# Rows 1 to 4 as one tile in an outer-product batch norm: a new order of tiles and one run for four rows

## The chip, the cores and the metric

The kernel runs on one core of a Trainium2 chip. The metric is the device time of one execution in microseconds (us); of several, the median is taken. The kernel before takes 1877.3 us (four runs, 1877.24 to 1877.37).

## What is computed

`r_xi` and `r_xj` hold 1024 samples of 39 fields of 16 numbers. For every pair of fields (row r, column c, c < r: 741 pairs) the 16 x 16 outer product is formed, normalised over the batch and the 256 places of that pair, scaled, and multiplied by a weight:

```python
cross = xj[:, rows, :, None] * xi[:, cols, None, :]
mean = jnp.mean(cross, axis=(0, 2, 3), keepdims=True)
var = jnp.mean(jnp.square(cross - mean), axis=(0, 2, 3), keepdims=True)
normed = (cross - mean) * jax.lax.rsqrt(var + BN_EPS)
normed = normed * gamma[None, :, None, None] + beta[None, :, None, None]
out = normed[:, :, None, :, :] * W[None, None, :, :, :]
```

The output is float32, 1024 x 741 x 256: 777 MB. In it, a sample's pairs lie row by row: row r has r pairs and begins at pair r(r-1)/2, so rows 1, 2, 3, 4 are pairs 0 to 9, next to each other. One pair is 1024 bytes.

## The kernel before

Samples lie on 128 partitions, eight on each. For about the first 35 us the inputs are loaded and mean and variance of all pairs are worked out from sums and a Gram matrix of the fields (TensorE, DVE, ACT, POOL); this gives for each pair a scale s (`st_sb[:, 0]`) and a shift t (`st_sb[:, 1]`). These are spread to all partitions in groups of rows (`ROW_GROUPS`); each group has a tile number at which its last three DVE steps (`apply`) are done.

Then the output is made in tiles. A tile is one row r for T = 2 samples of each partition, so each row has four tiles (sample pairs t0 = 0, 2, 4, 6) of 2 r pairs. The list `tiles` (lines 67 to 76) gives their order and their place in the buffer `y_sb`, which has two slots of 2 x 38 pairs. From row 38 down, a slot takes the tile of row r and, behind it, that of row 38 - r, so that it is full; then the other slot follows. First come rows 19, 20 and 18. The end is row 21 with row 17.

A tile passes three steps, and the main loop (lines 525 to 533) writes them out in the order that each engine keeps:

- `scale_xi` (L163): POOL multiplies xi by s into `xs` (L169), two tiles ahead; `xs` has two buffers.
- `products` (L177): for each of the two samples, 16 instructions multiply `xs` by one number of xj: 11 or 12 of them on ACT (L147), 5 or 4 on POOL (L149). They write all r pairs of that sample, so they wait until the stores of what lay there before have landed. For rows 1 to 4 (`SHORT`) DVE does it alone: one scaling (L182) and one product for each sample (L192).
- `finish` (L256): the shift is added and the weight multiplied, on DVE in one instruction for each pair and both samples (L293). Some pairs go elsewhere: in tiles of rows over 33 (`long`), ACT adds the shift of 8 pairs (L277) and POOL multiplies them, 4 pairs at a time (L282); in the others, POOL does both (L279, L282) for 13% of the pairs; in rows 1 to 4, DVE does all.

`store` (L205) then issues the runs on SP's queue (L216), which keeps their order. Rows over 30 go out in pieces (`bounds`), rows over 19 sample by sample, the others with both samples in one DMA. One DMA spreads over the 16 DMA engines; each run of one sample in one partition is one packet. Row 37 and row 38 go as a first piece of both samples and then a second piece for each; rows 36 to 31 as a first piece of sample 0, the rest of sample 0, and the whole of sample 1. A tile of row r can begin in a slot when sample 0's runs have left it, and finish its products when sample 1's have.

Of the kernel before, what the change touches and what calls it, by code (L numbers as in the profile page):

```python
# [7 lines left out]
F32 = mybir.dt.float32  # L8
AF = mybir.ActivationFunctionType
ALU = mybir.AluOpType  # L10
# [4 lines left out]
T = 2  # L15
# [3 lines left out]
ONE, LONG, WHOLE = 30, 33, 36  # L19
# [6 lines left out]
POOL_SHARE, POOL_PAIRS_LONG, POOL_PAIRS_FIRST = 0.13, 8, 3  # L26

LOADS = (1, 2, 3, 4, 6, 8)

SHORT, OWN = 4, 2  # L30


ROW_GROUPS = (
    (19, 20, 0, None), (20, 21, 1, None), (18, 19, 1, 2), (38, 39, 1, 8), (34, 38, 1, 9), (1, 5, 1, 10), (29, 34, 2, 36),
    (5, 10, 2, 37), (25, 29, 3, 76), (10, 14, 3, 77), (21, 25, 4, 108), (14, 18, 4, 109),
)
SHORT_GROUP = 5

# [2 lines left out]
def tile_pair_outer_batchnorm(  # L41
# [15 lines left out]
    nc = tc.nc  # L57
    P = nc.NUM_PARTITIONS
    NB, F, E = xi.shape
    NT = NB // P  # L60
    EE = E * E
    NP = F * (F - 1) // 2
    first = [r * (r - 1) // 2 for r in range(F)]

    half = T * (F - 1)
    mid = (F - 1) // 2
    tiles = [(mid, t0, t0 // T * half // 2) for t0 in range(0, NT, T)]
    slot = 0  # L70
    for r in (mid + 1, *range(F - 1, mid + 1, -1)):
        for t0 in range(0, NT, T):
            tiles.append((r, t0, slot * half))
            if r < F - 1:
                tiles.append((F - 1 - r, t0, slot * half + T * r))
            slot ^= 1

    RAW = 1

    cpool = ctx.enter_context(tc.tile_pool(name="cpool", bufs=1))  # L80
    scaled_short = ctx.enter_context(tc.tile_pool(name="scaled_short", bufs=1))
    scaled = ctx.enter_context(tc.tile_pool(name="scaled", bufs=2))
    psp = ctx.enter_context(tc.tile_pool(name="ps", bufs=1, space=bass.MemoryType.PSUM))
    xi_sb = cpool.tile([P, NT, F, E], F32, name="xi_sb")
# [47 lines left out]
    xj_short = ps_c.rearrange("p (t r i) -> p t r i", t=NT, i=E)  # L132
# [4 lines left out]
    def view(n):  # L137
        r, _, u = tiles[n]
        return y_sb[:, u : u + T * r, :].rearrange("p (t n) e -> p t n e", t=T)

    def product(n, engine, t, i, src):

        r, t0, _ = tiles[n]
        y = view(n).rearrange("p t n (i j) -> p t n i j", j=E)[:, t, :, i, :]
        scale = xj_sb[:, t0 + t, r, i : i + 1]
        if engine is nc.scalar:
            nc.scalar.activation(y, src, AF.Copy, scale=scale)  # L147
        else:
            engine.tensor_scalar(y, src, scale, 1.0, ALU.mult, ALU.mult)  # L149
# [7 lines left out]
    def emit(work, count):  # L157
        for _, step in zip(range(count), work):
            step()

    xs_of = {}

    def scale_xi(n):  # L163
        r, t0, _ = tiles[n]
        if r <= SHORT:
            return
        n0 = first[r]
        xs = scaled.tile([P, T, r, E], F32, tag="xs", name=f"xs_{r}_{t0}")
        nc.gpsimd.tensor_tensor(  # L169
            xs,  # L170
            xi_sb[:, t0 : t0 + T, 0:r, :],
            s_sb[:, :, n0 : n0 + r, :].to_broadcast([P, T, r, E]),
            ALU.mult,
        )
        xs_of[n] = xs

    def products(n):  # L177

        r, t0, _ = tiles[n]
        if r <= SHORT:  # L180
            xs = scaled_short.tile([P, T, r, E], F32, tag="xs_short", name=f"xs_{r}_{t0}")
            nc.vector.tensor_tensor(  # L182
                xs,
                xi_sb[:, t0 : t0 + T, 0:r, :],
                s_short[:, first[r] : first[r] + r]
                .unsqueeze(1)
                .unsqueeze(3)
                .to_broadcast([P, T, r, E]),
                ALU.mult,
            )  # L190
            for t in range(T):
                nc.vector.tensor_tensor(  # L192
                    view(n)[:, t].rearrange("p n (i j) -> p n i j", j=E),
                    xs[:, t].unsqueeze(2).to_broadcast([P, r, E, E]),
                    xj_short[:, t0 + t, r - 1 : r, :].unsqueeze(3).to_broadcast([P, r, E, E]),
                    ALU.mult,
                )
            return
        xs = xs_of.pop(n)
        split = E - (POOL_I_FIRST[n] if n < 3 else POOL_I_LONG if tiles[n][0] > LONG else POOL_I)  # L200
        for t in range(T):
            for i in range(E):
                product(n, nc.scalar if i < split else nc.gpsimd, t, i, xs[:, t])

    def store(n, c0, c1, t_from=0, t_to=T):  # L205
        r, t0, _ = tiles[n]
        n0 = first[r]

        whole = n >= len(FIRST_PIECES) and r <= WHOLE
        step = 1 if r > mid and (whole or c1 == r) else t_to - t_from  # L210
        for t in range(t_from, t_to, step):
            if whole and step == 1 and t == t_to - 1:
                if c1 < r:
                    continue
                c0 = 0
            nc.sync.dma_start(  # L216
                out_v[:, t0 + t : t0 + t + step, (n0 + c0) * EE : (n0 + c1) * EE],
                view(n)[:, t : t + step, c0:c1, :].rearrange("p t n e -> p t (n e)"),
            )
# [14 lines left out]
    def weigh(n):  # L234

        y = view(n)
        for c0, c1 in zip(bounds(n), bounds(n)[1:]):
            affine(n, range(c0, min(c1, OWN)), (nc.vector,))
            nc.vector.tensor_tensor(  # L239
                y[:, :, c0:c1, :],  # L240
                y[:, :, c0:c1, :],
                w_dve.unsqueeze(1).to_broadcast([P, T, c1 - c0, EE]),
                ALU.mult,
            )
            store(n, c0, c1)

    def bounds(n):
        if n < len(FIRST_PIECES):
            return FIRST_PIECES[n]
        r = tiles[n][0]  # L250
        if r <= ONE:
            return 0, r

        return 0, r // 2 + max(0, (WHOLE + 1 - r) * 3 // 2), r

    def finish(n):  # L256


        r = tiles[n][0]
        n0 = first[r]  # L260
        y = view(n)
        long = r > LONG
        p1 = r // 2 if long else r
        if long:
            share = POOL_PAIRS_LONG
        elif RAW < n < 10:
            share = POOL_PAIRS_FIRST
        else:
            share = int(r * POOL_SHARE + 0.5) if r > SHORT else 0
        p0 = p1 - share  # L270
        step = POOL_PAIRS_LONG // 2 if long else r
        for c0 in range(p0, p1, step):
            c1 = min(c0 + step, p1)
            for c in range(c0, c1):
                t_c = t_sb[:, n0 + c : n0 + c + 1]
                if long:
                    nc.scalar.activation(y[:, :, c, :], y[:, :, c, :], AF.Identity, bias=t_c)  # L277
                else:
                    nc.gpsimd.tensor_scalar(  # L279
                        y[:, :, c, :], y[:, :, c, :], t_c, 1.0, ALU.add, ALU.mult  # L280
                    )
            nc.gpsimd.tensor_tensor(  # L282
                y[:, :, c0:c1, :],
                y[:, :, c0:c1, :],
                w_sb.unsqueeze(1).to_broadcast([P, T, c1 - c0, EE]),
                ALU.mult,
            )

        size = 1 if n == RAW else T
        for t in range(0, T, size):  # L290
            for c0, c1 in zip(bounds(n), bounds(n)[1:]):
                for c in [*range(c0, min(c1, p0)), *range(max(c0, p1), c1)]:
                    stt(  # L293
                        y[:, t : t + size, c, :],
                        y[:, t : t + size, c, :],
                        t_sb[:, n0 + c : n0 + c + 1],
                        w_dve.to_broadcast([P, size, EE]),
                        ALU.add,
                        ALU.mult,
                    )  # L300
                store(n, c0, c1, t, t + size)

    with tc.manual_schedule():
# [209 lines left out]

        affine(0, range(OWN, 12))
        scale_xi(1)
        affine(0, range(12, mid))
        weigh(0)
        for group in range(1, len(ROW_GROUPS)):
            spread(group)
        s_short = spread_of[SHORT_GROUP][0][:, 0]  # L520
        apply(1)
        products(1)
        scale_xi(2)

        for n in range(1, len(tiles)):
            if n + 2 < len(tiles):
                scale_xi(n + 2)
            finish(n)
            for group, (_, _, _, tile_of) in enumerate(ROW_GROUPS):
                if n == tile_of:  # L530
                    apply(group)
            if n + 1 < len(tiles):
                products(n + 1)
            if n == 12:
                nc.scalar.copy(xj_short, xj_sb[:, :, 1 : SHORT + 1, :])
# [28 lines left out]
```

## Time and profile before

| | us |
|---|---|
| median of four runs | 1877.3 |
| profiled execution | 1877.23 |
| its span, first to last instruction | 1875.5 |
| DVE busy | 1723.9 |
| ACT busy | 1647.3 |
| POOL busy | 1535.6 |
| store queue's packets, share of 16 DMA engines over the span | 98.1% |

In the page, part 1 has each engine's busy time, part 2 the span in 40 slices (busy share in tenths; GB/s moved), part 3 the DMA queues. q1 is the queue of the loads and stores that SP issues, q10 ACT's loads, q14 the fetching of instructions. In a row of a group or of the timeline, "128x528" is partitions x elements, "xN" a count; the bracket or the part behind the second bar tells the idle time ahead of it and what ended it. A row of an answer on waits reads: who waited, for what, us in total, times, the longest. A row of a DMA issue ends in the time from the issue to the landing on the last of the 16 engines.

### The profile page before, as it was taken

The numbers are of one execution on the slowest core, as the hardware profiler recorded it, in microseconds if no ns is written. First come the engines' busy times: TensorE is split into PE (matmuls) and PEld (weight loads), VectorE is DVE, ScalarE is ACT, GpSimd is POOL, SyncE is SP. The second block draws the span as 40 slices with busy tenths as digits, with TensorE's granted clock in tenths as the row PEclk, the third lists the DMA queues.
The fourth block names the chain that finished last, engine by engine and source line by source line (L and its number), as shares of the span: only waits on it lengthen the run. The fifth ranks groups of instructions, "written<-read, shape, count | busy, mean of one in ns | idle before, by whom it ended". The sixth has DMA issues, their size and how long they took to land. (4 is left out here: it accounts for less than half of the span.)

```text
span 1875.5 us, 9638 instructions
## 1 busy us (share of the span) xinstructions
PE 26.0 (1%) x130; PEld 23.3 (1%) x130; DVE 1723.9 (92%) x2640; ACT 1647.3 (88%) x3416; POOL 1535.6 (82%) x1746
## 2 busy tenths in 40 slices
PE   4000000000000000000000000000000000000000
PEld 4000000000000000000000000000000000000000
DVE  8999888899999999999999999999999999999994
ACT  7999888898888899989999999998999998989892
POOL 8999877787777788888888888888888888888882
DMA  5999999999999999999999999999999999999998
GB/s 198 387 422 419 431 424 425 426 425 426 425 426 425 426 426 426 431 426 420 424 425 432 426 425 432 425 425 432 425 430 425 430 426 429 426 428 431 427 428 349
DMA packets 54714, 783.63 MB, mean 418 GB/s; under 512 B 4720, under 2 KB 6384, under 8 KB 17520
## 3 DMA queue, kind: packets, MB, share of 16 engines
q1 hardware_dynamic: 53344, 779.72, 98.1%
q10 hardware_dynamic: 1296, 3.29, 0.5%
q14 instruction: 73, 0.60, 0.1%
q8 instruction: 1, 0.02, 0.0%
HBM read 6.00 MB, written 776.99 MB: 417 GB/s over the span
## 5 line engine op out<-in xcount | busy, mean ns | idle before, releaser
L293 DVE SCALAR_TENSOR_TENSOR y_sb<-y_sb,st_sb,w_dve 128x512 f32<-128x512 f32 (+1 forms) x2511 | 1653.2, 740 | 115.3 <-issue 101.4
L147 ACT ACTIVATE y_sb<-xs,xj_sb 128x288 f32<-128x288 f32 (+20 forms) x3194 | 1515.6, 581 | 177.7 <-DMA out_dram<-y_sb 145.9
L149 POOL TENSOR_SCALAR y_sb<-xs,xj_sb 128x480 f32<-128x480 f32 (+27 forms) x1126 | 607.2, 565 | 8.4 <-DMA out_dram<-y_sb 8.4
L282 POOL TENSOR_TENSOR y_sb<-y_sb,w_sb 128x2048 f32<-128x2048 f32 (+3 forms) x155 | 517.7, 3346 | 89.9 <-ACT y_sb L277 80.3
L169 POOL TENSOR_TENSOR xs<-xi_sb,st_sb 128x640 f32<-128x640 f32 (+33 forms) x135 | 184.2, 1364 | 198.1 <-ACT y_sb L147 194.3
L279 POOL TENSOR_SCALAR y_sb<-y_sb,st_sb 128x512 f32<-128x512 f32 x291 | 197.6, 695 | 5.1 <-ACT y_sb L147 5.1
L277 ACT ACTIVATE y_sb<-y_sb,st_sb 128x512 f32<-128x512 f32 x160 | 100.3, 711 | 4.0 <-POOL y_sb L149 2.3
L192 DVE TENSOR_TENSOR y_sb<-xs,ps 128x256 f32<-128x256 f32 (+3 forms) x32 | 24.8, 818 | 0.6
L491 PE MATMUL ps<-y_sb 39*128 39x38 f32 (+37 forms) x76 | 16.4, 397 | 2.8 <-DVE y_sb L477 2.8
L491 PEld LDWEIGHTS ps<-y_sb 39*128 39x128 f32 x76 | 16.3, 329 | 3.1 <-DVE y_sb L477 3.1
L355 ACT ACTIVATE y_sb<-y_sb 128x1248 f32<-128x1248 f32 x8 | 10.0, 1245 | 2.8 <-POOL y_sb L344 2.4
L360 DVE TENSOR_REDUCE y_sb<-y_sb 128x78 f32<-128x1248 f32 x8 | 11.2, 1446 | 0.3 <-ACT y_sb L355 0.3
L147 ACT ACTIVATE y_sb<-xi_sb,xj_sb 128x304 f32<-128x304 f32 x24 | 11.4, 540 | 0.0
L344 POOL TENSOR_TENSOR y_sb<-xi_sb,y_sb 128x1248 f32<-128x1248 f32 x4 | 9.2, 2321 | 2.4 <-ACT y_sb L393 2.4
L239 DVE TENSOR_TENSOR y_sb<-y_sb,w_dve 128x2048 f32<-128x2048 f32 (+4 forms) x6 | 10.7, 1839 | 0.1
L334 DVE TENSOR_REDUCE y_sb<-xi_sb 128x39 f32<-128x624 f32 (+1 forms) x6 | 6.1, 1012 | 3.9 <-DMA xi_sb<-in_r_xi_dram 3.9
L344 POOL TENSOR_TENSOR y_sb<-xj_sb,y_sb 128x1248 f32<-128x1248 f32 x4 | 9.2, 2320 | 0.0
L380 PE MATMUL ps<-y_sb 128*39 128x79 f32 x48 | 8.0, 340 | 15.3 <-DVE y_sb L360 15.1
L232 POOL TENSOR_SCALAR y_sb<-y_sb,st_sb 128x512 f32<-128x512 f32 x8 | 6.5, 816 | 2.1 <-ACT y_sb L147 2.1
L334 DVE TENSOR_REDUCE y_sb<-xj_sb 128x39 f32<-128x624 f32 (+1 forms) x6 | 6.1, 1016 | 0.9 <-DMA xj_sb<-in_r_xj_dram 0.9
L230 ACT ACTIVATE y_sb<-y_sb,st_sb 128x512 f32<-128x512 f32 x9 | 6.5, 804 | 0.2 <-ACT y_sb L147 0.2
L380 PEld LDWEIGHTS ps<-y_sb 128*39 128x39 f32 x48 | 5.8, 178 | 17.3 <-DVE y_sb L360 10.5
(59 smaller groups left out, 37.5 us busy)
## 6 DMA issues: line engine op xcount, KB each, us to landing
out_dram<-y_sb SPq DMA_DIRECT2D x16, 3072.0 KB, 21.9
out_dram<-y_sb SPq DMA_DIRECT2D x20, 2432.0 KB, 12.5
out_dram<-y_sb SPq DMA_DIRECT2D x10, 4608.0 KB, 15.1
out_dram<-y_sb SPq DMA_DIRECT2D x12, 3840.0 KB, 21.6
out_dram<-y_sb SPq DMA_DIRECT2D x16, 2816.0 KB, 22.3
out_dram<-y_sb SPq DMA_DIRECT2D x12, 3584.0 KB, 23.1
out_dram<-y_sb SPq DMA_DIRECT2D x12, 3328.0 KB, 24.3
out_dram<-y_sb SPq DMA_DIRECT2D x15, 2560.0 KB, 11.9
```

The source lines that it names most:

```text
L147: nc.scalar.activation(y, src, AF.Copy, scale=scale)
L149: engine.tensor_scalar(y, src, scale, 1.0, ALU.mult, ALU.mult)
L169: nc.gpsimd.tensor_tensor(xs, xi_sb[:, t0 : t0 + T, 0:r, :], s_sb[:, :, n0 : n0 + r, :].to_broadcast([P, T, r, E]), ALU.mult,)
L192: nc.vector.tensor_tensor(view(n)[:, t].rearrange("p n (i j) -> p n i j", j=E), xs[:, t].unsqueeze(2).to_broadcast([P, r, E, E]), xj_short ...
L277: nc.scalar.activation(y[:, :, c, :], y[:, :, c, :], AF.Identity, bias=t_c)
L279: nc.gpsimd.tensor_scalar(y[:, :, c, :], y[:, :, c, :], t_c, 1.0, ALU.add, ALU.mult)
L282: nc.gpsimd.tensor_tensor(y[:, :, c0:c1, :], y[:, :, c0:c1, :], w_sb.unsqueeze(1).to_broadcast([P, T, c1 - c0, EE]), ALU.mult,)
L293: stt(y[:, t : t + size, c, :], y[:, t : t + size, c, :], t_sb[:, n0 + c : n0 + c + 1], w_dve.to_broadcast([P, size, EE]), ALU.add, ALU.mult,)
L334: nc.vector.tensor_reduce(total[:, t0:t1, part(x)], sources[x][:, t0:t1], AX.X, ALU.add)
L344: nc.gpsimd.tensor_tensor(devs[n % 7], sources[x][:, t0 : t0 + T], shift[:, x : x + 1, :].unsqueeze(3).to_broadcast([P, T, F, E]), ALU.sub ...
L380: nc.tensor.matmul(ps_g[acc][0:F, 0 : 2 * F + 1], lhs, fb[:, t], start=t == 0, stop=t == NT - 1)
L491: nc.tensor.matmul(ps[:, :, first[r] - n0 : first[r] - n0 + r], pick[:, r, :], stq[:, :, 0:r], start=True, stop=True,)
```

## The change

The tiles get another order, and rows 1 to 4 become one.

- Rows 1 to 4 of a sample pair are one tile of 10 pairs (`grouped`; row number 0 in the list of short tiles, 10 in `tiles`). DVE makes the four rows' products as before, one after another, into that tile; `finish` does its 10 pairs on DVE; its store is one DMA in which a run is 10 pairs long, from pair 0.
- Rows 37, 36, 35, 34 have no short tile behind them. Rows 33 to 29 keep rows 5 to 9. In each of rows 28, 27, 26, 25 the first sample pair's slot takes a grouped tile; the other three slots take the tiles of rows 10, 11 and 12 in order (10, 10, 10 beside 28; 10, 11, 11 beside 27; 11, 11, 12 beside 26; 12, 12, 12 beside 25). Rows 24 to 21 take rows 13 to 16, so their slots hold 37 pairs a sample.
- Row 17's four tiles come last, two in each slot.
- The long tile beside a grouped one (`beside`) is finished as rows over 33 are: 8 pairs over ACT and POOL.
- In `ROW_GROUPS` six tile numbers are changed to suit the order.

```diff
 ROW_GROUPS = (
-    (19, 20, 0, None), (20, 21, 1, None), (18, 19, 1, 2), (38, 39, 1, 8), (34, 38, 1, 9), (1, 5, 1, 10), (29, 34, 2, 36),
-    (5, 10, 2, 37), (25, 29, 3, 76), (10, 14, 3, 77), (21, 25, 4, 108), (14, 18, 4, 109),
+    (19, 20, 0, None), (20, 21, 1, None), (18, 19, 1, 2), (38, 39, 1, 8), (34, 38, 1, 9), (1, 5, 1, 10), (29, 34, 2, 26),
+    (5, 10, 2, 27), (25, 29, 3, 64), (10, 14, 3, 65), (21, 25, 4, 96), (14, 18, 4, 97),
 )
...
-    tiles = [(mid, t0, t0 // T * half // 2) for t0 in range(0, NT, T)]
+    rest = SHORT * (SHORT + 1) // 2
+    samples = range(0, NT, T)
+    tiles = [(mid, t0, t0 // T * half // 2) for t0 in samples]
+    short = [(mid - 1, t0) for t0 in samples]
+    short += [(r, t0) for r in range(SHORT + 1, rest) for t0 in samples]
+    late = [(r, t0) for r in range(rest, mid - 2) for t0 in samples]
+    for q, t0 in enumerate(samples):
+        late.insert(4 * q, (0, t0))
+    short += late
+
+    grouped, beside = set(), set()
     slot = 0
     for r in (mid + 1, *range(F - 1, mid + 1, -1)):
-        for t0 in range(0, NT, T):
+        for t0 in samples:
             tiles.append((r, t0, slot * half))
-            if r < F - 1:
-                tiles.append((F - 1 - r, t0, slot * half + T * r))
+            if r < F - SHORT - 1 and (short[0][0] or rest) < F - r:
+                row, t1 = short.pop(0)
+                if not row:
+                    beside.add(len(tiles) - 1)
+                    grouped.add(len(tiles))
+                tiles.append((row or rest, t1, slot * half + T * r))
             slot ^= 1
+    for q, t0 in enumerate(samples):
+        tiles.append((mid - 2, t0, (slot ^ q // 2) * half + q % 2 * T * (mid - 2)))
...
+    def base(n):
+        return 0 if n in grouped else first[tiles[n][0]]
...
-        if r <= SHORT:
-            xs = scaled_short.tile([P, T, r, E], F32, tag="xs_short", name=f"xs_{r}_{t0}")
...
-            for t in range(T):
+        if n in grouped:
+            for row in range(1, SHORT + 1):
+                pairs = slice(first[row], first[row] + row)
+                xs = scaled_short.tile([P, T, row, E], F32, tag="xs_short", name=f"xs_{row}_{t0}")
                 nc.vector.tensor_tensor(
...
+                for t in range(T):
+                    nc.vector.tensor_tensor(
+                        view(n)[:, t, pairs].rearrange("p n (i j) -> p n i j", j=E),
+                        xs[:, t].unsqueeze(2).to_broadcast([P, row, E, E]),
+                        xj_short[:, t0 + t, row - 1 : row, :].unsqueeze(3).to_broadcast([P, row, E, E]),
+                        ALU.mult,
+                    )
             return
...
     def store(n, c0, c1, t_from=0, t_to=T):
         r, t0, _ = tiles[n]
-        n0 = first[r]
+        n0 = base(n)
...
-        n0 = first[r]
+        n0 = base(n)
         y = view(n)
-        long = r > LONG
+        long = r > LONG or n in beside
...
-            share = int(r * POOL_SHARE + 0.5) if r > SHORT else 0
+            share = 0 if n in grouped else int(r * POOL_SHARE + 0.5)
```

More of the change, by code (lines that the diff above doesn't have):

```diff
@@ L68, in tile_pair_outer_batchnorm @@
     mid = (F - 1) // 2
-    tiles = [(mid, t0, t0 // T * half // 2) for t0 in range(0, NT, T)]
+    rest = SHORT * (SHORT + 1) // 2
[8 more added lines that the diff above has]
+    grouped, beside = set(), set()
     slot = 0
     for r in (mid + 1, *range(F - 1, mid + 1, -1)):
-        for t0 in range(0, NT, T):
+        for t0 in samples:
             tiles.append((r, t0, slot * half))
-            if r < F - 1:
-                tiles.append((F - 1 - r, t0, slot * half + T * r))
+            if r < F - SHORT - 1 and (short[0][0] or rest) < F - r:
[4 more added lines that the diff above has]
+                tiles.append((row or rest, t1, slot * half + T * r))
             slot ^= 1
+    for q, t0 in enumerate(samples):
+        tiles.append((mid - 2, t0, (slot ^ q // 2) * half + q % 2 * T * (mid - 2)))
+    assert not short
     RAW = 1
@@ L179, in products @@
         r, t0, _ = tiles[n]
-        if r <= SHORT:
-            xs = scaled_short.tile([P, T, r, E], F32, tag="xs_short", name=f"xs_{r}_{t0}")
[L182 to L190, printed above, removed]
-            for t in range(T):
+        if n in grouped:
+            for row in range(1, SHORT + 1):
+                pairs = slice(first[row], first[row] + row)
+                xs = scaled_short.tile([P, T, row, E], F32, tag="xs_short", name=f"xs_{row}_{t0}")
                 nc.vector.tensor_tensor(
-                    view(n)[:, t].rearrange("p n (i j) -> p n i j", j=E),
-                    xs[:, t].unsqueeze(2).to_broadcast([P, r, E, E]),
-                    xj_short[:, t0 + t, r - 1 : r, :].unsqueeze(3).to_broadcast([P, r, E, E]),
+                    xs,
+                    xi_sb[:, t0 : t0 + T, 0:row, :],
+                    s_short[:, pairs].unsqueeze(1).unsqueeze(3).to_broadcast([P, T, row, E]),
                     ALU.mult,
                 )
+                for t in range(T):
[5 more added lines that the diff above has]
+                    )
             return
```

## The prediction

> **What bounds the kernel now.** I read the page first: the span, the busy engines, the DMA slices, the queues.
>
> ```profile
> span 1875.5 us, 9638 instructions
> PE 26.0 (1%) x130; PEld 23.3 (1%) x130; DVE 1723.9 (92%) x2640; ACT 1647.3 (88%) x3416; POOL 1535.6 (82%) x1746
> DMA  5999999999999999999999999999999999999998
> GB/s 198 387 422 419 431 424 425 426 425 426 425 426 425 426 426 426 431 426 420 424 425 432 426 425 432 425 425 432 425 430 425 430 426 429 426 428 431 427 428 349
> q1 hardware_dynamic: 53344, 779.72, 98.1%
> ```
>
> The store queue q1 holds the 16 DMA engines for 98.1% of the span. DVE is busy for 92%, yet it is not the bound, as the waits show:
>
> ```profile
> ACT y_sb L147 <- DMA out_dram<-y_sb: 145.9, 81, 4.4
> DVE y_sb L293 <- issue: 101.4, 70, 5.2
> ```
>
> ACT waits 81 times until a store has left the slot that it wants to fill. So the time is the packets' time plus the moments in which no store is queued. How near those are is seen in the timeline where tile 33 takes the slot of tile 34:
>
> ```profile
> 613.82 17.21 DVE L293 SCALAR_TENSOR_TENSOR y_sb<-y_sb,st_sb,w_dve 128x512 f32<-128x512 f32 x26 [1.39 <-issue]
> 616.52 9.03 POOL L282 TENSOR_TENSOR y_sb<-y_sb,w_sb 128x2048 f32<-128x2048 f32 x2 [4.43 <-ACT y_sb L277]
> 629.43 21.20 ACT L147 ACTIVATE y_sb<-xs,xj_sb 128x528 f32<-128x528 f32 x48 [2.56 <-DMA out_dram<-y_sb]
> 637.14 21.82 DVE L293 SCALAR_TENSOR_TENSOR y_sb<-y_sb,st_sb,w_dve 128x512 f32<-128x512 f32 x33 [0.77 <-issue]
> ```
> ```profile
> 636.39 0.38 SPq L216 DMA_DIRECT2D out_dram<-y_sb  x1
> ```
> ```profile
> out_dram<-y_sb SPq DMA_DIRECT2D x1, 1024.0 KB, 19.1
> ```
> ```profile
> 651.86 0.33 SPq L216 DMA_DIRECT2D out_dram<-y_sb  x1
> ```
>
> Row 34's last run frees the slot at 629.4. ACT makes the second sample's 12 products in 7.6 us, DVE starts at 637.14 and needs 22 pairs at 0.661 (21.82/33), and SP issues at 651.86: 22.4 us after the slot came free. The store ahead of it, row 4's, was issued at 636.39 and landed 19.1 later, at 655.5. I call the difference, 3.6 us, the lead. What lead is enough is read from the trace's packet gaps: leads (against the engine that landed first) of 0.49, 0.62, 0.78, 0.84 and 0.94 us left holes of 0.71, 0.60, 0.42, 0.42 and 0.28. So a lead below about 1.2 us costs 1.2 minus the lead.
>
> **What the joined run saves.** The trace's packet records by size, one packet being one run of one sample and partition:
>
> ```
> bytes   1024   2048   3072   4096   10240
> ns      48.2   86.8  123.8  163.1   390.6
> ```
>
> Four packets, 421.9 ns, become one of 390.6: 31.3 ns less for each of 1024 samples, over 16 engines 2.0 us. Sixteen stores become four; each ends with a 9 ns packet on each engine: 12 x 9 ns = 0.1. All engines carry the same bytes, and the last to finish sets the end: a store's 16 landings lie 0.2 us apart at 200 us and 8.6 at the end, so I reckon with the last one. **-2.1 us**.
>
> Here a rule speaks against the change. The Trainium skill, DMA: Bandwidth & Descriptors, section Specifications, gives 512 B as the smallest transfer at line rate, and its section on why small descriptors are slow finds joining them worthwhile only up to 256 B; by that the saving would be nothing and the sum 1881.6. The row says otherwise: 1024 B in 48.2 ns is 21 bytes a ns, 10240 B in 390.6 is 26.
>
> **What lone rows 37 to 34 cost.** The short tiles' stores were also time in the queue, between a slot's release and the next need of it. The release-to-issue chain has none of their work: it goes through ACT (L147, L277), POOL (two products of 4.5 us, L282) and DVE on the long tile, and ACT does nothing for rows 1 to 4. So without them each lead shrinks by those stores that lay in its window, two as a rule. A store of row 1, 2, 3, 4 takes 16 packets an engine: 0.78, 1.40, 1.99, 2.62 us. From the trace's issue and last landing:
>
> ```
> tile (sample pair)       lead before   short stores in it   left
> 37 (2nd, 3rd, 4th)       2.2 2.8 2.6   0.8 1.6 1.6          1.4 1.2 1.0
> 36 first                 4.0           1.6                  2.4
> 36 2nd: run 1, run 2     3.0 2.0       2.2                  0.8 -0.2
> 36 3rd, 4th              4.9 6.2       2.8                  2.1 3.4
> 35 (four)                5.9 5.3 5.7 6.8   2.8 3.4 4.0 4.0  3.1 1.9 1.7 2.8
> 34 (four)                5.8 6.6 7.1 6.2   4.0 4.6 5.2 5.2  1.8 2.0 1.9 1.0
> 33 first                 3.6           5.2                  -1.6
> 33 2nd                   2.9           2.6                  0.3 + hole before
> ```
>
> Holes against 1.2: 37's fourth 0.2; 36's second 0.4, and 1.0 more at its second run (its lead is -0.2 plus the 0.4 just lost); 34's fourth 0.2; 33's first 2.8, since it is the one place where a chain of 22.4 us meets a window of one lone tile (20.9). 33's second has that 2.8 in its window: 3.1, no hole. Sum 4.6; a hole lengthens the next window too, so I take the two of 0.2 at half: **+4.4 us**. Behind the late issue on SP stand only the same tile's runs; on ACT the bias adds and the next tile's products wait for the same slot. Bounds: 0 (leads are last landings of a queue with some tenths of scatter; the 38 rows stand alone already, with 1.5 to 4.2 left and no hole on the last engine) and 10 (all leads 0.8 lower). I take the table's value: the tiles in it are the very ones that stand alone now, and lone 38 is only one pair away from lone 37.
>
> **What the tile of rows 1 to 4 costs beside 28 to 25.** DVE makes its products in a row:
>
> ```profile
> L192 DVE TENSOR_TENSOR y_sb<-xs,ps 128x1024 f32<-128x1024 f32 x8 | 9.4, 1218 | 0.1
> L192 DVE TENSOR_TENSOR y_sb<-xs,ps 128x768 f32<-128x768 f32 x8 | 7.3, 951 | 0.1
> L192 DVE TENSOR_TENSOR y_sb<-xs,ps 128x512 f32<-128x512 f32 x8 | 5.1, 684 | 0.1
> L192 DVE TENSOR_TENSOR y_sb<-xs,ps 128x256 f32<-128x256 f32 x8 | 3.0, 418 | 0.1
> ```
>
> 24.8 us over four sample pairs is 6.2 a tile, with the scaling (L182, 3.7 in all) 7.1; then 10 pairs, 6.6. The neighbour 28 goes the long way (8 pairs to ACT and POOL): 20 pairs on DVE, 13.2. The slot has 27.0 us of DVE against 23.4 of store time (38 pairs; 23.3 between the landings of tiles 28). Before, it had 33 pairs, 21.8. The first store of 28 goes out 2.7 earlier (20 pairs, not 24): its lead rises from 6.0 to 8.7. The next 28 then has 8.7 + 23.4 - (7.1 + 6.6 + 15.9) = 2.5: above 1.2, no hole. The three slots up to the next such tile win back 1.5 each (21.9 of DVE). At 27, 26 and 25 the leads of before were larger (7.4 to 9.6): **0**. ACT gains 8 adds of 0.63 and loses row 10's products there; POOL's two products of 4.5 end before DVE's 13.2. Bounds: 0, and once the cover of 1.3 (2.5 less 1.2) is gone, whatever is beyond it up to four times: 4 if DVE takes 2.3 longer a tile.
>
> **The rest at nothing.** The six due tiles of the scale groups move with the order: the same three DVE steps of 0.3 us, in stages where DVE idles 1 to 3 us a tile. Row 17 last: 15 pairs, 9.9 us of DVE, against 10.5 of store time, with leads of 13 to 19 us there; the last store is the same 4352 KB. ACT's 32 more instructions of 3416 are a quarter of one fetch packet (309 ns) on q14.
>
> **Sum.** The profiled execution is 1877.23 (span 1875.5 and 1.7 around it), 0.07 under the median: 1877.23 - 2.1 + 4.4 = **1879.5**. That is within 0.2% (3.75 us) of before, about what a measurement of this kernel can tell from no change.
>
> **Rivals.** (1) The holes don't come: the lag of the late engines is taken up by idle time of the others, and only the saving stays: 1875.2. For it: rows 38 alone show none on the last engine. Against: 33's first tile is short by 2.8, not by tenths. Chance 0.18. (2) Slower: the lone rows are short of work at every tile. Place: L282 on POOL, whose 9 us after ACT's adds end just at the first store. If the chains are 0.8 us longer than before (the scaling of the next tile, L169, now stands in front of them at every tile), the right column gives holes of 10; half of the small ones lie in each other's windows: 8, so 1883.1. It decides from some 0.3 us a tile. Chance 0.16. (3) DVE becomes the bound beside 28 to 25: two more us there lose up to 4: 1883. For it: 27.0 against 23.4; against: three lighter slots follow. Chance 0.06. (4) A gain over 0.2% would need more than the saving, say a shorter lag of the last engine at the end: 1873. Chance 0.03. The forecast has 0.57, its own range 1877.4 to 1881.0.
>
> **Range and chances.** From (1)'s 1875.2 to within (2) and (3): 1875.1 to 1882.6. Faster 0.03; slower 0.22, (2) and (3); same 0.75, the forecast and (1).
>
> **What would show it.** Packets under 2 KB number 5168 (6384 - 1024 - 12 x 16), stores 267 (279 - 12); a hole of 2 to 3 us stands before 33's first store and one of about a us in 36's second; none beside 28. Wrong it is if holes stand at every lone tile, or after each grouped one, or none at 33.

## The result: 3.6 us longer, and the profile after

The changed kernel takes 1880.87 us (median; 1880.43 to 1881.69) beside 1877.25 for the kernel before in the same comparison: a ratio of 1.0019, 95% interval 1.0015 to 1.0024. Run again beside the last of the experiments, it took 1880.69 against 1877.23, again 1.0019 (1.0010 to 1.0028). So it is slower by 3.5 to 3.6 us, just inside the 0.2% (3.75 us) that the prediction had set as the limit of "no change". The forecast was 1879.5. The profiled execution took 1880.43, its span is 1878.7.

The page of the changed kernel: span, engines, DMA slices, small packets, store queue.

```profile
span 1878.7 us, 9574 instructions
PE 26.0 (1%) x130; PEld 23.3 (1%) x130; DVE 1710.5 (91%) x2622; ACT 1665.0 (89%) x3448; POOL 1543.1 (82%) x1736
GB/s 200 387 418 424 431 428 421 422 414 429 433 427 421 402 425 425 428 428 425 424 428 429 425 413 426 428 428 428 424 429 430 426 426 427 428 429 427 428 428 365
DMA packets 51450, 783.63 MB, mean 417 GB/s; under 512 B 4528, under 2 KB 5168, under 8 KB 13232
q1 hardware_dynamic: 50080, 779.72, 97.8%
```

Packets under 2 KB are 5168, as foreseen, and the store queue's share fell from 98.1% to 97.8%. The fourteenth slice (611 to 658 us) moved 402 GB/s; before it was 426. DVE is busy for 13.4 us less than before and the time is longer all the same, so it isn't the sum of DVE's work that sets it. ACT is busy for 17.7 us more, but it also waits longer for stores, 161.0 us in all instead of 145.9:

```profile
ACT y_sb L167 <- DMA out_dram<-y_sb: 161.0, 88, 4.2
DVE y_sb L315 <- issue: 132.8, 62, 5.1
```

The place in the fourteenth slice is row 33's first tile. From the timeline: ACT, DVE and POOL on it, then SP's issue of its first store, and last the last run of row 34 ahead of it (issued at 613.15), whose row ends in the time to its last landing.

```profile
608.95 34.74 ACT L167 ACTIVATE y_sb<-xs,xj_sb 128x528 f32<-128x528 f32 x84 [0.89 <-DMA out_dram<-y_sb]
616.65 29.06 DVE L315 SCALAR_TENSOR_TENSOR y_sb<-y_sb,st_sb,w_dve 128x512 f32<-128x512 f32 x44 [3.91 <-issue]
621.45 4.53 POOL L304 TENSOR_TENSOR y_sb<-y_sb,w_sb 128x2048 f32<-128x2048 f32 x1
```
```profile
613.15 1.02 SPq L238 DMA_DIRECT2D out_dram<-y_sb  x1
```
```profile
out_dram<-y_sb SPq DMA_DIRECT2D x1, 4352.0 KB, 16.5
```
```profile
631.37 0.33 SPq L238 DMA_DIRECT2D out_dram<-y_sb  x1
```

The slot is free at 608.95, DVE starts at 616.65, the store is issued at 631.37: 22.4 us, the same as before. But the queue ran dry at 613.15 + 16.5 = 629.7, so the lead is -1.7 us; before it was 3.6. From here on "hole" is the time between two neighbouring stores' landings that is more than the packets of the second take, read from the trace's issue and landing records. A store lands 16 times, once on each DMA engine; "first" is the engine that lands first, "last" the one that lands last.

The places that the prediction had named, in us:

```
place                          predicted   first   last engine
37, fourth tile                   0.1       0        0
36, second tile, first run        0.4       0.6      0
36, second tile, second run       1.0       1.03     1.05
34, fourth tile                   0.1       0        0
33, first tile                    2.8       3.2      3.05
28, second tile                   0         2.55     0.04
```

The last engine has 4.1 us of holes, where the prediction had 4.4 and put them in the same places. The first engine has three more where the prediction had none: 0.9 at 37's second tile, 0.6 at the second run of 36's first tile and 0.6 at 34's third tile. On the last engine there is none at these three. Beside row 28, DVE's row is unbroken through the grouped tile's products (here those of row 4) into 45 pairs:

```profile
1099.26 2.35 DVE L214 TENSOR_TENSOR y_sb<-xs,ps 128x1024 f32<-128x1024 f32 x2
1101.53 29.71 DVE L315 SCALAR_TENSOR_TENSOR y_sb<-y_sb,st_sb,w_dve 128x512 f32<-128x512 f32 x45
```

DVE has no idle time there, the next tile's first store goes out at 1124.14, and the lead is 2.2 us on the last engine (predicted 2.5), -1.35 on the first. So the engines that run ahead do have a hole, and the one that is behind has none.

If the holes are as predicted and the difference is about 1.3 larger than its sum of 2.3, the joined run must have saved less than the 2.1 us it was booked at. The experiments ask that first, then whether the holes are the whole loss, and what the way of finishing beside the grouped tiles is worth.

### The profile page after: what moved, and what is told of

Its sections match the earlier page's. It is cut to its first block, busy times and chain, and to the rows that moved or that the text cites. A ratio compares the mean times of both kernels' runs of the same rounds, so it can differ in the third digit from the quotient of the medians.

```text
span 1878.7 us, 9574 instructions
## 1 busy us (share of the span) xinstructions
PE 26.0 (1%) x130; PEld 23.3 (1%) x130; DVE 1710.5 (91%) x2622; ACT 1665.0 (89%) x3448; POOL 1543.1 (82%) x1736
## 2 busy tenths in 40 slices
DMA packets 51450, 783.63 MB, mean 417 GB/s; under 512 B 4528, under 2 KB 5168, under 8 KB 13232
## 3 DMA queue, kind: packets, MB, share of 16 engines
q1 hardware_dynamic: 50080, 779.72, 97.8%
## 5 line engine op out<-in xcount | busy, mean ns | idle before, releaser
L315 DVE SCALAR_TENSOR_TENSOR y_sb<-y_sb,st_sb,w_dve 128x512 f32<-128x512 f32 (+1 forms) x2493 | 1639.0, 740 | 136.2 <-issue 132.8
L167 ACT ACTIVATE y_sb<-xs,xj_sb 128x288 f32<-128x288 f32 (+25 forms) x3194 | 1514.0, 567 | 167.9 <-DMA out_dram<-y_sb 161.0
L304 POOL TENSOR_TENSOR y_sb<-y_sb,w_sb 128x2048 f32<-128x2048 f32 (+3 forms) x159 | 537.5, 3387 | 40.8 <-ACT y_sb L299 31.5
L301 POOL TENSOR_SCALAR y_sb<-y_sb,st_sb 128x512 f32<-128x512 f32 x277 | 187.4, 692 | 7.0 <-ACT y_sb L167 6.6
L299 ACT ACTIVATE y_sb<-y_sb,st_sb 128x512 f32<-128x512 f32 x192 | 120.2, 708 | 4.2 <-POOL y_sb L169 2.2
L254 POOL TENSOR_SCALAR y_sb<-y_sb,st_sb 128x512 f32<-128x512 f32 x8 | 6.4, 814 | 2.2 <-ACT y_sb L167 2.2
L252 ACT ACTIVATE y_sb<-y_sb,st_sb 128x512 f32<-128x512 f32 x9 | 6.5, 800 | 0.2 <-ACT y_sb L167 0.2
## 6 DMA issues: line engine op xcount, KB each, us to landing
out_dram<-y_sb SPq DMA_DIRECT2D x16, 2816.0 KB, 19.8
```

Source lines behind the costliest of these rows:

```text
L301: nc.gpsimd.tensor_scalar(y[:, :, c, :], y[:, :, c, :], t_c, 1.0, ALU.add, ALU.mult)
L304: nc.gpsimd.tensor_tensor(y[:, :, c0:c1, :], y[:, :, c0:c1, :], w_sb.unsqueeze(1).to_broadcast([P, T, c1 - c0, EE]), ALU.mult,)
L315: stt(y[:, t : t + size, c, :], y[:, t : t + size, c, :], t_sb[:, n0 + c : n0 + c + 1], w_dve.to_broadcast([P, size, EE]), ALU.add, ALU.mult,)
```

## The experiments

Each kernel ran beside the kernel before on the same chip; the last columns are the difference to that (us) and the ratio. Chips differ by some tenths, so kernels are compared by these differences. Where two intervals overlap (the changed kernel with e1, e2, e5 and e8, and e9 with e10), the times alone do not tell the two apart, and what is said of them rests on their landings as well.

```
kernel                                  us        diff    ratio (95% interval)
changed kernel                          1880.87   +3.6    1.0019 (1.0015 to 1.0024)
e1  four runs instead of one            1881.37   +3.9    1.0022 (1.0013 to 1.0031)
e8  ten runs instead of one             1883.26   +6.3    1.0033 (1.0021 to 1.0046)
e2  33's first tile as rows over 33     1883.94   +6.5    1.0035 (1.0022 to 1.0049)
e3  two of 33's tiles so, 36 recut      1885.99   +8.6    1.0046 (1.0033 to 1.0059)
e5  33's first store 3 pairs later      1882.78   +5.4    1.0029 (1.0019 to 1.0040)
e6  before, 33's first store later      1879.43   +2.5    1.0013 (1.0004 to 1.0022)
e7  33 to 31: POOL's pairs earlier      1877.32   +0.4    1.0002 (0.9993 to 1.0011)
e9  e7, row 37 sample by sample         1876.73   -0.2    1.0000 (0.9991 to 1.0009)
e10 e9 with four runs                   1877.57   +0.3    1.0002 (0.9993 to 1.0011)
e11 e9 with 33's first run shorter      1877.29   +0.1    1.0000 (0.9991 to 1.0009)
e4  no other finish beside              1887.98  +10.8    1.0058 (1.0045 to 1.0070)
e12 changed kernel, again               1880.69   +3.5    1.0019 (1.0010 to 1.0028)
```

The last row is the changed kernel once more, so that e4, e10 and e11 have it on their chip:

> The changed kernel itself, on the chip and beside the runs of e4, e10 and e11, so that their differences to it are free of the tenths by which chips differ. Both theories: 1880.9, 0.19% above the kernel before on the same chip.

### Undoing the join alone (e1)

The grouped tile stays as it is, but is stored by four DMAs, rows 1, 2, 3, 4.

```diff
+        if n in grouped and (c0, c1) == (0, r):
+            for row in range(1, SHORT + 1):
+                store(n, first[row], first[row] + row, t_from, t_to)
+            return
```

> The changed kernel with its joined tile stored as four DMAs, one for each of rows 1 to 4 (runs of 1, 2, 3, 4 KB), and nothing else moved. Theory (the packets set the time, joining saved 31.3 ns a sample and 12 closing packets): 2.1 us longer than the changed kernel's 1880.9, so 1883.0. Rival (runs from 512 B up go at line rate, joining saved nothing and the 3.6 us are holes alone): 1880.9 to 1881.0.

It took 1881.37, 0.3 to 0.5 us more than the changed kernel by the differences to the kernel before, not 2.1 (2.1 more would lie just inside e1's interval, whose upper end is 1.0031). The trace tells why. For each of the four grouped tiles, the time from the landing of the store ahead of it to its own last landing was taken, once by the first of the 16 landings and once by the last (means of the four tiles, us):

```
                          first engine   last engine
four stores (e1)              6.65           6.33
one store (changed kernel)    6.18           6.18
difference, four tiles        1.9            0.6
```

On the engines that are ahead, the join saves 1.9 us over the kernel, as its packets' mean times had said. On the engine that lands last, which sets the end, the same four stores take only 6.33 a tile, and the join saves 0.6. Its packets are somewhat shorter there: where an engine runs behind the others, packets of 1, 2, 3 and 4 KB took 46, 84, 121 and 159.6 ns in the trace (410.6 together) against 48.2, 86.8, 123.8 and 163.1 in the mean over the kernel before (421.9). For the 16 of each that an engine takes in a tile that is 0.18 us, about half of the 0.32 between 6.65 and 6.33; the other half is not explained.

The prediction's own traces could have said so: in the kernel before, the four short stores take 0.62, 1.25, 1.86 and 2.40 us by the last landing (means without one of the row 2 stores, which took 2.1 us), 6.12 in all, and 6.33 with that store. By that the join saves between nothing and 0.6 us over the four tiles.

### Ten runs, to enlarge the effect (e8)

```diff
+        if n in grouped and (c0, c1) == (0, r):
+            for c in range(r):
+                store(n, c, c + 1, t_from, t_to)
+            return
```

> The changed kernel with the joined tile stored as ten DMAs of one pair each (1 KB runs). By the mean packet times: 10 x 48.2 instead of 390.6 ns, 91 ns x 64 = 5.9 us, and 36 more closing packets, 0.3: 1887.1. By the times of a late engine's packets (46.0 and 387.7 ns): 72 ns x 64 = 4.6 and 0.3, 1885.8. If the time hangs on these packets only in part, as the 0.5 us of the four runs suggest (a quarter of 2.1): about 1882.5.

1883.26: 2.7 to 2.9 above the changed kernel, by the differences. By mean packets it should have been 6.2. Again the landings part: a store of 1 KB runs took 0.76 us by the first landing and 0.69 by the last (medians of the forty). Ten of them take 7.6 us by the first landing in three of the four tiles (8.15 in the first, where the queue ran dry in between), and 6.68 to 7.42 by the last, 6.98 in the mean, against 6.18. Over four tiles that is 5.7 on the first engine and 3.2 on the last; the measured 2.8 is near the second. None of the three expected figures came: 2.8 lies between the one for a quarter of the packets' time (1.6 more than the changed kernel) and the one by a late engine's packets (4.9), and the one by mean packets (6.2) lies outside the interval. Meanwhile the engines that are ahead used up the hole that they had beside row 28: it shrank from 2.55 to 1.0 us, half of it among the small stores themselves.

### The same without the holes (e10)

One doubt was left: the holes might hide the saving. e10 is e9 (below), in which the large holes are gone, with the four stores of e1.

> The kernel of the run e9 (the changed kernel without its large holes: 1876.7 us) with the grouped tile stored as four DMAs again, rows 1, 2, 3, 4 one after another. Of the join's worth e1 left open whether 2.1 us are there and the holes before it take them, or whether they never come. If the joined run is worth its packet time (2.1) when no store is late, this kernel takes 1876.7 + 2.1 = 1878.8. If it is worth only the 0.5 to 0.9 that e1 showed, holes or not, it takes 1877.2 to 1877.6.

Its difference to the kernel before is +0.3, that of e9 -0.2: the join is worth about 0.5 us here too, as far as so small a difference can be read. Its four tiles take 6.33 us by the last landing, the same as in e1. Holes or not, it never came to 2.1.

### Giving 33's first tile more hands (e2, e3)

In e2, row 33's first tile is finished as the rows over 33 are: ACT adds the shift of 8 pairs, POOL multiplies them.

```diff
-        long = r > LONG or n in beside
+        long = r > LONG or n in beside or n == 32
```

> The changed kernel with row 33's first tile finished as the rows over 33 are (8 pairs over ACT and POOL): its first run is due 11.8 us after the products, not 14.6. Theory (a hole of 3.05 us stands ahead of this store on all engines): that lead goes from -1.7 to about 1.2 and the hole is gone; the next tile of row 33 loses the slack that the hole gave it (lead 3.9 to 0.8, a hole of 0.4): 1880.9 - 2.7 = 1878.2. Rival (the time is lost all along the lone rows or beside the grouped tiles, where DVE has 27 us a slot): under 1 us gained, 1880 or more.

This expectation failed: 1883.94. The hole at 33's first tile did go, from 3.05 to 0.7, but one of 4.97 came at its second tile. ACT's rows from e2's timeline, then DVE's, then the issue of the second tile's first store:

```profile
616.66 5.02 ACT L299 ACTIVATE y_sb<-y_sb,st_sb 128x512 f32<-128x512 f32 x8
621.59 48.94 ACT L167 ACTIVATE y_sb<-xs,xj_sb 128x80 f32<-128x80 f32 x121
```
```profile
616.66 19.18 DVE L315 SCALAR_TENSOR_TENSOR y_sb<-y_sb,st_sb,w_dve 128x512 f32<-128x512 f32 x29 [3.92 <-issue]
642.84 27.74 DVE L315 SCALAR_TENSOR_TENSOR y_sb<-y_sb,st_sb,w_dve 128x512 f32<-128x512 f32 x42 [7.00 <-issue]
```
```profile
657.57 0.33 SPq L238 DMA_DIRECT2D out_dram<-y_sb  x1
```

The eight adds stand 5.02 us on ACT ahead of row 5's and the next tile's products, and ACT has no idle time behind them (121 instructions with no gap). So the next tile's products are late, DVE idles 7.0 us until 642.84 (in the changed kernel its row runs through from 616.65 to 660.2), and the hole has moved one tile on. By holes e2 should be 4.97 + 0.7 - 3.05 = 2.6 over the changed kernel; it is 3.0.

e3 does the same to 33's second tile too, and gives row 36 a first run of 23 pairs:

```diff
+        if r == WHOLE:
+            return 0, 23, r
...
-        long = r > LONG or n in beside
+        long = r > LONG or n in beside or n in (32, 34)
```

> As before it, with row 33's second tile finished that way too, and row 36's first run 23 pairs long instead of 19, so that its second run (lead 0.3, hole 1.05) has more queued ahead of it. Theory: holes of 3.05 and 1.05 are both gone and the saving of 2.1 stays, 1880.9 - 4.1 = 1876.8, below the kernel before (1877.25); lag that an engine had when a hole brought all engines into step is no longer kept, which may give up to 1 more. Rival (other losses, along lone rows or beside grouped tiles): 1879 or more.

1885.99, another miss of the same kind: holes of 0.75, 1.9 and 6.4 at 33's first, second and third tile. ACT has no time to give in this stage.

### Lengthening the chain on purpose (e5, e6)

e5 lets 33's first store wait for 25 pairs instead of 22; e6 does the same in the kernel before, with 28 pairs, where the lead was 3.6 us.

```diff
+        if n == 32:
+            return 0, 25, r
```
```diff
+        if n == 48:
+            return 0, 28, r
```

> The changed kernel with the first run of row 33's first tile 25 pairs long instead of 22: DVE's three more pairs issue it 2.0 us later, nothing else is moved. Theory (each us past a lead of 1.2 is lost on all engines for good): 2.0 us longer, 1882.9. Rival (a hole here is taken up later by slack): 1880.9.

> The kernel before, with the first run of row 33's first tile 28 pairs long instead of 22: DVE's six more pairs issue it 4.0 us later. Theory (a lead down to 1.2 us is free, what is missing below it is lost): the lead goes from 3.6 to -0.3, a hole of 1.5: 1878.8. Rival (any delay of this store costs its own length): 1881.2. Rival (DMA has slack enough): 1877.3.

e5 is 1.7 to 1.9 over the changed kernel, for an issue 2.3 us later (633.7): where the queue is already dry, a delay is paid in most of its length. e6 is 2.5 over the kernel before, for an issue 3.6 us later (655.4 after 651.9), so neither figure expected of it came: the theory had 1.5 and the rival that a delay costs its own length had 4. The lead became -0.3 us on the last engine and the hole 1.74, as the rule of 1.2 less the lead says (1.5). On the first engine the lead went from 1.7 to -2.25 and the hole was 3.46. The cost lies between these two, so 0.7 more than the last engine's hole explains. Of the 3.6 us some 1.1 were free; by the last engine's lead alone it should have been 2.4. So the lead was cover, which the moved short stores had given, but less of it than the last engine's figure says.

On the engine that lands first, the rule of 1.2 less the lead holds to within about 0.1 us, for 130 stores with a lead under 1.1 us in the traces of all kernels here. Leads of 0.54, 0.15, -1.35 and -1.99 us in the changed kernel, -2.25 in e6 and -3.94 in e5 left holes of 0.64, 1.03, 2.55, 3.2, 3.46 and 5.2.

### Taking the holes away (e7, e9, e11)

In rows 33 to 31 POOL finishes four pairs at the end of the tile. e7 moves them to the end of the first run, so that DVE has 18 pairs, not 22, ahead of the first store; and row 36's first run has 22 pairs, not 19.

```diff
+        if r == WHOLE:
+            return 0, 22, r
...
-        p1 = r // 2 if long else r
+        p1 = r // 2 if long else bounds(n)[1] if ONE < r <= LONG else r
```

> The changed kernel; in rows 33 to 31 the four pairs that POOL finishes are the last of the first run, not of the tile, so DVE has 18 pairs ahead of the first store and not 22, 2.6 us less, and no engine gets work; row 36's first run is 22 pairs. Theory (the holes of 3.05 and 1.05 are the whole loss, and the first try failed only because the adds that it gave to ACT delayed the next tile's products): holes of about 0.3 and 0.5 are left, 1880.9 - 3.3 = 1877.6. Rival (a hole filled here opens at the next tile whatever is done): 1880 or more.

1877.32, or 3.1 us off the changed kernel's loss of 3.5. POOL was idle when needed, unlike ACT, so nothing is late at the next tile. 33's first store goes out at 627.85, 3.5 earlier:

```profile
627.85 0.33 SPq L238 DMA_DIRECT2D out_dram<-y_sb  x1
```

Its lead is 0.98 on the last engine and a hole of 1.04 is left, more than the 0.2 of the rule. On the first engine it is as the rule says, a lead of 0.67 and a hole of 0.5. At the same store the landings spread from 0.3 to 0.86 us, so about half of the 1.04 is one engine falling behind, and not the late issue. 36's second tile keeps 0.65 in two parts.

e9 adds that row 37 is stored sample by sample like row 36, so that a slot's first sample has left it after 37 pairs' runs instead of 55 and the next tile's products can start sooner:

```diff
-        whole = n >= len(FIRST_PIECES) and r <= WHOLE
+        whole = n >= len(FIRST_PIECES) and r <= WHOLE + 1
...
-        if r == WHOLE:
+        if r in (WHOLE, WHOLE + 1):
             return 0, 22, r
```

> As with POOL's pairs first, and row 37 stored sample by sample with a first run of 22 pairs, as row 36 is, so that its slot is released one sample earlier. Theory: the hole at row 36's second tile (0.5 left) goes, 1877.1. Rival (the windows of row 37 get shorter at their second runs): 1878 or more.

1876.73, level with the kernel before (1876.94 on that chip). 36's holes are gone; a hole of about 0.8 at 37's second tile and one of 1.05 at 33's first (0.5 on the first engine) are left. In the timeline, row 33's first tile now stands like this (two added lines move L315 to L317):

```profile
607.49 42.25 ACT L167 ACTIVATE y_sb<-xs,xj_sb 128x528 f32<-128x528 f32 x96 [0.89 <-DMA out_dram<-y_sb]
615.19 34.98 DVE L317 SCALAR_TENSOR_TENSOR y_sb<-y_sb,st_sb,w_dve 128x512 f32<-128x512 f32 x53 [3.91 <-issue]
```
```profile
627.28 0.33 SPq L238 DMA_DIRECT2D out_dram<-y_sb  x1
```

From the free slot to the issue it is 19.8 us instead of 22.4. Summed row by row, the last engine's landings put the whole gain where the holes were: from the changed kernel to e9 the stores of rows 36 and 33 take 2.0 and 2.3 us less, those of row 37 0.5 more, and all others together the same. In e7 rows 36 and 33 take 0.9 and 2.3 less, and all others the same. So the loss of the changed kernel sits at these few places: without most of the holes it is as fast as before within the interval, with the join still in. The holes that went add up to less than the gain, though, 2.4 us of 3.1 in e7 and 2.25 of 3.7 in e9, and what the rest is made of is not shown.

e11 tried to win the last 1.05 by a shorter first run of row 33:

```diff
+        if r == WHOLE - 3:
+            return 0, 21, r
```

> The kernel of the run e9 with 21 pairs instead of 22 in the first run of row 33's tiles. Its first store there had a lead of 0.94 us on the last engine and left a hole of 1.05; issued one pair (0.66) sooner its lead is 1.6 and the hole 0.3 or less, while the second run, with a lead of 1.63, loses about the length of one pair's store (0.3) and keeps 1.3. Theory: 0.7 less than e9, 1876.0, which would be below the kernel before. Rival: what is won there is lost again at row 33's next tiles or lies in the lag of the last engine: 1876.7.

No gain: 0.1 over the kernel before, against 0.2 under it for e9, which is nothing beside the intervals. The lead of the first run rose to 1.63 as meant, but that of the second fell from 1.63 to 0.81, with a hole of 0.6. The second run waits for the whole of the sample pair's work, which did not become less. No version here beats both kernels by more than a measurement can tell.

### The finish beside the grouped tiles (e4)

The prediction had booked the grouped tiles at nothing because the long tile beside each gives 8 pairs to ACT and POOL. Here it does not:

```diff
-        long = r > LONG or n in beside
+        long = r > LONG
```

> The changed kernel with the long tile beside a grouped one finished as its neighbours are (24 pairs on DVE, 4 on POOL) instead of the way of rows over 33. Beside 28 DVE has 4 pairs, 2.65 us, more before the first grouped tile, so the second tile of row 28 starts with a lead of 6.0 + 23.4 - (7.1 + 6.6 + 15.9) = -0.2 instead of 2.2 on the last engine: a hole of 1.4. The second tiles of 27, 26 and 25 keep 3.7, 4.5 and 4.8 less 2.65, so 1.0 to 2.1, with 0.2 at the first. Theory: 1880.9 + 1.6 = 1882.5. Rival: the fast engines' idle time there (2.55 already in the changed kernel) is all that grows, and the last engine, which sets the end, loses nothing: 1880.9.

1887.98, 7.3 over the changed kernel on the same chip (e12). The direction was right and the size far off. The 24th, 28th and 30th slices of its page, which hold the second tiles of rows 28, 26 and 25, are low, at 385, 410 and 392:

```profile
GB/s 200 387 421 422 429 427 418 426 413 433 426 431 423 398 427 424 430 425 423 428 430 423 431 385 425 423 426 410 424 392 429 425 428 431 425 427 429 427 428 389
```

ACT waits for stores up to 9.1 us at a time, in the changed kernel up to 4.2:

```profile
ACT y_sb L167 <- DMA out_dram<-y_sb: 179.7, 88, 9.1
```

DVE's row beside row 28 starts on the pairs 3.0 us later than in the changed kernel, and so does the issue:

```profile
1104.53 27.07 DVE L315 SCALAR_TENSOR_TENSOR y_sb<-y_sb,st_sb,w_dve 128x512 f32<-128x512 f32 x41
```
```profile
1127.15 0.33 SPq L238 DMA_DIRECT2D out_dram<-y_sb  x1
```

The leads (last engine) at the second tiles of rows 28, 27, 26 and 25, and the holes:

```
row                          28      27      26      25
lead, changed kernel         2.2     3.7     4.5     4.8
lead, e4                    -0.4     0.9     0.0    -1.7
less by                      2.6     2.8     4.5     6.5
hole, e4                     1.8     0.5     1.4     3.1
```

At row 28 it went as expected (a lead of -0.2 and a hole of 1.4 were). The expectation then took 2.65 off each of the other three, as if the rows in between won the loss back. At row 27 that holds (2.8), at 26 and 25 it does not: DVE has 24 pairs to do where it had 20, the loss is carried on, and the holes add up to 6.8 of the 7.3. From 1090 to 1470 us DVE is busy for 379.0 us of 380, in the changed kernel for 375.5, in the kernel before for 357.9. Here DVE is the bound, which is the prediction's third rival at the place that it named. The finish of the neighbour is what keeps the changed kernel off it, and narrowly.

## Why the prediction came out as it did

**The holes: right.** "Holes against 1.2" gave 4.4 us at six places. 33's first tile has 3.05 for 2.8, 36's second run 1.05 for 1.0; the small ones did not come on the last engine (0.6 predicted in all). Together 4.1. e7 and e9 show that the loss sits at these places: filling most of the holes takes off 3.1 and then 3.7 us of the 3.5 to 3.6, all of it at rows 36 and 33, where the holes that went add up to 2.4 and 2.25. One thing was mixed: the rule of 1.2 had been read against the engine that lands first and the table's leads against the one that lands last. On the first engine the rule holds (e5, e6 and the places above), and there are holes where the table had none. That the last engine's sum came so near is partly that at 33 and at 36's second run the engines were together, within 0.3 and 0.2 us.

**The grouped tiles beside 28 to 25 at 0: right, and its cover was named right.** The lead at 28's second tile is 2.2 where 2.5 was predicted, on the last engine. e4 takes the cover away: 7.3 us. The prediction's upper bound of 4 for that place assumed 2.3 us too much a tile, each paid once after the cover of 1.3; in e4 the deficit of DVE did not stay the same from row to row, it grew (leads 2.6, 2.8, 4.5 and 6.5 less).

**The joined run at -2.1: the term that was mis-sized.** The step that failed is "31.3 ns less for each of 1024 samples, over 16 engines 2.0 us". The prediction said itself that the last engine sets the end and that the landings spread up to 8.6 us apart, and then priced the saving with packet times averaged over all engines. By the last engine's landings the saving is between nothing (short stores of the kernel before, 6.12 a tile without the one long store, against 6.18) and 0.6 (e1, 6.33 against 6.18); undoing it costs 0.3 to 0.5 with the holes and 0.5 without them (e1, e10), and making it ten times small runs costs 2.8 where mean packets say 6.2 (e8). With 4.1 of holes and 0 to 0.6 of saving the sum is 3.5 to 4.1; the measured difference is 3.5 to 3.6. So close a fit is partly luck: on the last engine the stores of rows 5 to 9 took 1.5 us more than before and those of rows 32, 34 and 35 2.4 less, which neither term covers.

The rule set against the row, in the Trainium skill, DMA: Bandwidth & Descriptors, section on why small descriptors are slow, finds putting consecutive descriptors into one packet worthwhile only up to 256 B. It does not speak of one longer run in place of four, which is what the change makes. What the prediction drew from it, no saving and 1881.6, is nearer to the 1880.9 than the prediction's own sum. The landings say that it is not so for each engine: on an engine that is ahead, ten 1 KB stores took 7.6 us for the joined store's 6.18. The gain is there and is spent in waiting for the last engine.

**The rivals.** (1), holes that the late engines' lag takes up, is what happened beside row 28 (2.55 on the first engine, 0.04 on the last, no cost), but not at 33, where all engines run dry within 0.3 us of each other. (2), short at every lone tile, did not come: 12 of the 16 leads at rows 37 to 34 are larger than the table's, and only that of 36's second run (0.31) is below 1.2. (3) is shown real by e4; in the changed kernel DVE has next to no idle time there, but the last engine has no hole. (4): the lag at the end did become shorter, 5.9 us instead of 8.5, but by the engines ahead coming later; the last one gained nothing.

**What stays open.** Why the engine that is behind gets its small stores through more quickly is not shown by any record here, and its shorter packets account for about half of it; that it does is shown. In e6 0.7 us of the loss lies between the first and the last engine's hole, and no run tells how the two combine.

## What to carry to other kernels

Where a queue is always full, as here, work taken out of it is not free: the stores that were moved away were the cover for the slot's next chain, and each tile that loses them must be asked for its lead, the last landing ahead less its own issue. Price a saving in the queue by the landings of the engine that finishes last, and not by mean packet times; what the other engines won here they waited away. Read the lead and the rule for it on the same engine. A hole that is filled must be filled with an engine that has idle time there: POOL had it and the hole went, ACT had not and the hole came back one tile later and larger.

## What the runs showed of the hardware that was not expected

- Stores of small runs take less on the engine that lands last than on the others: 0.69 us against 0.76 for 256 runs of 1 KB over 16 engines (e8), 6.33 against 6.65 for runs of 1 to 4 KB together (e1). For runs of 10 KB both take 6.18.
- The 16 engines drift apart while the queue stays full, to 8.5 us at the end of the kernel before and 5.9 at the end of the changed one; a hole gathers them again. At row 28's second tile the spread falls from 3.6 to 1.0 us in the changed kernel and to 0.2 in e4. So a hole that only the engines ahead saw cost the last one nothing there (0.04 us for a lead of -1.35 on the first), while at 33, where the engines were together, a lead of -1.7 cost it 3.05.
- Part of the drift comes in steps. From row 38 on, the spread grew by more than 0.3 us from one store's landings to the next 21 times in the kernel before and 11 times in the changed one, by up to 1.2. Each time a packet of q14, the fetching of instructions (309 ns in the median), began between the first landing of the store ahead and the last of this one; without a step that was so for about 3 stores in 11. The 2.1 us store of row 2 and the half of e7's and e9's last hole at 33 are such steps. That a fetch holds up the one engine that carries it is a reading: the records do not name a packet's engine.
